# Cross-attention units of a Perceiver layer: the row of maxima on another queue, value products placed later, and the last unit's exponentials

## The chip, the cores and the metric

The kernel runs on one core of a Trainium2 chip. A core has five engines that follow their own instruction streams and meet at semaphores: TensorE (PE, matrix products; its weight loads are listed apart as PEld), VectorE (DVE), ScalarE (ACT), GpSimd (POOL) and SyncE (SP), which computes nothing and issues most of the transfers. ACT can issue transfers as well. Every engine takes its instructions in program order: one that waits holds back all that stand behind it on that engine.

The metric is the device time of one execution in microseconds, the median of several runs.

## The reference

One Perceiver layer over 16 batches of 64 latent rows (1024 wide): cross-attention to a context of 1024 rows for each batch, then self-attention with rotary embedding, then a feed-forward with quantized weights. The change touches the cross-attention and the first steps behind it.

```python
def xattn(query, key, value, Wq, Wk, Wv, Wo):      # 32 heads of 32, 8 key/value heads
    q = (query @ Wq).reshape(b, sq, 32, 32).transpose(0, 2, 1, 3)
    k = (key @ Wk).reshape(b, sk, 8, 32).transpose(0, 2, 1, 3)
    v = (value @ Wv).reshape(b, sk, 8, 32).transpose(0, 2, 1, 3)
    k, v = jnp.repeat(k, 4, axis=1), jnp.repeat(v, 4, axis=1)
    scores = jnp.einsum('bhqd,bhkd->bhqk', q, k) * 32 ** -0.5
    out = jnp.einsum('bhqk,bhkd->bhqd', jax.nn.softmax(scores, -1), v)
    return out.transpose(0, 2, 1, 3).reshape(b, sq, 1024) @ Wo

x = x + xattn(layernorm(x), ctx, ctx, Wq, Wk, Wv, Wo)
x = x + attn(layernorm(x), wq, bq, wk, bk, wv, bv)
x = x + ffn(layernorm(x), w_gate, w_up, w_down, s_gate, s_up, s_down)
```

The context is given transposed, so that its products need no transposition on the chip.

## The kernel before

All data are float32 in one large buffer that the program places by hand (`arena`; the profile names nearly every tile so). The order of instructions is the order of the program text: no scheduler moves anything. PSUM tiles for projections come from a pool of two buffers (`m_tile`), the score tiles from two buffers `w0` and `w1`.

**Units.** The cross-attention is cut into 32 units (class `Unit`, L416). Unit n is batch n // 2 and head group n % 2 (four key/value heads, jj 0 to 3, each shared by four query heads: 256 columns, that is 4 heads x 64 rows). The scores of a unit are held transposed, keys on the partitions, in four quarters of 256 keys. The methods are these:

- `by_key(i)` (L421): eight matmuls for quarter i into `w0` and `w1` (profile: PE t L430), then ACT copies both halves into the quarter's buffer (L442) and DVE keeps the running maximum over the keys, element by element, in `most` (L446 for quarter 0, L449 for the others).
- `reduce` (L451): DVE transposes and reduces `most` to one maximum for each of the 1024 columns (L454 to L461), as a 32 x 32 tile `turned_top`.
- `spread` (L465) writes that tile to a row of DRAM, `tops`, 4 KB; `everywhere` (L469) reads the row back into all 128 partitions as `shift_by`, 512 KB. The second waits for the first to land. Both are issued by ACT. Two rows alternate.
- `exponentials(i)` (L472): DVE subtracts `shift_by` from quarter i (L475), ACT takes the exponential (L476), POOL adds it to `acc`, the sum over keys (L479 for the first addition, L482 for the other six).
- `values(waves)` (L484): 16 matmuls for two quarters, exponentials times values (PE o L491).
- `finish` (L499): four matmuls with ones give the sums (PE o L501), then DVE divides (L508, L513 or L515) and POOL copies one half (L518).

**The unit loop (L919 to L985).** The loop's unit n has its scores already; while its exponentials and value products run, the scores of unit n + 1 (`following`) are made. One pass has four steps i, one for each quarter. Between them the program takes work from a list, `fillers`, with `fill()`: two pieces a step, eight a unit. For units 0 to 29 the list holds the projections of the next batch's context: for an even n its first 512 keys, for an odd n the other 512. They are four half products for the keys (PE k L225; two halves make one product of eight matmuls, copied by ACT at L305) and then four blocks for the values (PE v L311, eight matmuls each, copied by ACT at L318), so that the steps 0 and 1 fill with keys, the steps 2 and 3 with values. For units 30 and 31 it holds 16 halves of the output projection (`project_out`, PE wo L225, with a residual addition on DVE, L529) for the rows of tiles 4, 5, 0 and 1 and, behind tiles 0 and 1, their second layer norm (`norm2`: DVE L170 to L174, POOL L176, DVE L162). `norm2` writes to the places of `most` and `shift_by`.

**Behind the loop (L986 on).** The rest of the list, then the output projections of tiles 2 and 3 with the transpositions of the normed tiles (`transpose2`, PE n2p L260), three pieces of which go ahead of the last unit's `finish`; then tiles 6 and 7, the self-attention and the feed-forward.

**Other transfers.** SP issues the context halves (`load_context`, L207 for all loads by `load`; 2 MB each, two stream buffers, so a load waits for PE to have read the one before the last), the rows of x (L203), and the pieces of the feed-forward's weights, 688 KB each (`load_piece`, L369). Such a piece is treated by ACT on its way through the loop (`treat_piece`, L372): in a first round its magnitudes are summed (L377), in a second it is made ternary (L381, L385), written back by SP (L386), and the piece after the next is loaded. Treatments stand in every step up to unit 7, later in steps 0 and 2, and in step 3 of odd units. Their instructions on ACT stand between the score copies and the projections' copies.

**The start.** The query projections of both halves come first (PE q L225); unit 0's scores are made between the last of them. Then come `spread`, `load_context(1, 0)`, and `everywhere` of unit 0, and four value blocks of batch 0 in a row, before step 0 of unit 0 begins with the keys of batch 1.

Of the kernel before, what the change touches and what calls it, by code (L numbers as in the profile page):

```python
# [20 lines left out]
P = 128  # L21
# [6 lines left out]
HD = 32  # L28
# [21 lines left out]
def kernel(  # L50
# [21 lines left out]
    nc = tc.nc  # L72
# [17 lines left out]
    def m_tile(name):  # L90
        return ps_m.tile([P, 512], F32, tag="m", name=name)
# [4 lines left out]
    def place(kb, shape, dtype=F32):  # L96

        first, n = round(kb * 256), math.prod(shape) * mybir.dt.size(dtype)
        a = arena[:, first : first + (n + 3) // 4]
        if dtype != F32:  # L100
            a = a.bitcast(dtype)
        a = a[:, : math.prod(shape)]
        if len(shape) > 1:
            names = [f"a{i}" for i in range(len(shape))]
            sizes = dict(zip(names[1:], shape[1:]))
            a = a.rearrange(f"p ({' '.join(names)}) -> p {' '.join(names)}", **sizes)
        return a
# [47 lines left out]
    tops = [dram.tile([1, 1024], F32, name=f"tops{i}") for i in range(2)]  # L155

    def layernorm(dst, src, name):

        made = []
        return [  # L160
            lambda: made.append(layernorm_scale(src, name)),
            lambda: nc.vector.tensor_scalar(  # L162
                dst, src, made[0][0][:, 0:1], made[0][1], ALU.subtract, ALU.mult
            ),
        ]
# [26 lines left out]
    shift_by = place(176, [1024])  # L192
# [6 lines left out]
    turned_top = place(195.25, [HD])  # L199
    quarters = most[:, 0:P].rearrange("p (i q) -> p i q", i=4)  # L200

    def load_x(dst, t):
        nc.sync.dma_start(dst, x[bass.ts(t, P), :])  # L203
# [13 lines left out]
    def matmul_steps(out, lhsT, rhs, done):  # L217

        made = []

        def piece(first):
            if first:
                made.append(out())
            for k in range(0, 4) if first else range(4, KC):
                nc.tensor.matmul(  # L225
                    made[0], lhsT=lhsT(k), rhs=rhs(k), start=(k == 0), stop=(k == KC - 1)
                )
            if not first:
                done(made[0])

        return [lambda: piece(True), lambda: piece(False)]
# [22 lines left out]
    def transposed(dst, xn, name, tile, engines):  # L254

        for i in range(2):
            tp = tile(f"{name}_{i}")
            tp = tp.rearrange("p (k q) -> p k q", k=4)
            for k in range(4):
                nc.tensor.transpose(tp[:, k, :], xn[:, bass.ts(i * 4 + k, P)], ident)  # L260
            if engines[i] == "act":
                nc.scalar.copy(dst[i], tp)  # L262
            else:
                nc.vector.tensor_copy(dst[i], tp)
# [25 lines left out]
    def load_context(b, h):  # L290
        ctx_halves[b, h] = load(ctxT[b, h])
# [66 lines left out]
    def half_of(a, c):  # L358
        return a[:, (c % 2) * HALF : (c % 2 + 1) * HALF]
# [5 lines left out]
    def load_piece(i):  # L365
        if i < 2 * len(pieces_of_w):
            m, c = pieces_of_w[i % len(pieces_of_w)]
            st = ws_ring.next([HALF])
            nc.sync.dma_start(st, weight_source(m, c))  # L369
            loaded.append((i, m, c, st))  # L370

    def treat_piece():  # L372
        if not loaded:
            return
        i, m, c, st = loaded.pop(0)
        if i < len(pieces_of_w):
            nc.scalar.activation(st, st, AF.Abs, accum_out=asum[:, m, c : c + 1])  # L377
        else:


            nc.scalar.activation(  # L381
                st, st, AF.Identity, scale=inverse[:, m : m + 1], bias=magic[:, 0:1]
            )
            q = place(ternary_at, [HALF], F8)
            nc.scalar.activation(q, st, AF.Sign, bias=magic[:, 1:2], saturate=False)  # L385
            nc.sync.dma_start(half_of(ternary[m][c // 2], c), q)  # L386
        if i + 2 not in (len(pieces_of_w), len(pieces_of_w) + 1):
            load_piece(i + 2)
# [27 lines left out]
    class Unit:  # L416
# [47 lines left out]

        def spread(self):  # L465
            row = tops[self.n % 2]
            nc.scalar.dma_start(row.rearrange("o (n c) -> (o n) c", n=HD), turned_top[0:HD])

        def everywhere(self):  # L469
            nc.scalar.dma_start(shift_by, tops[self.n % 2].to_broadcast([P, 1024]))  # L470

        def exponentials(self, i):  # L472
            pt = self.pts[i]
# [49 lines left out]
    def project_out(t, h):  # L523
        cols = bass.ts(h, 512)
        return matmul_steps(
            lambda: m_tile(f"wo_{t}_{h}"),
            lambda k: outputs[k // 4][:, t, k % 4, :, :],
            lambda k: wos[h][:, k, :],
            lambda ps: nc.vector.tensor_tensor(xs[t][:, cols], ps, xs[t][:, cols], ALU.add),  # L529
        )  # L530
# [20 lines left out]
    def norm2(t):  # L551
        n2s[t] = n2_ring.next([DIM])
        for step in layernorm(n2s[t], xs[t], f"n2_{t}"):
            step()

    def transpose2(t, tile):
        half, tl = t // 4, t % 4
        cols = bass.ts(tl, P)
        transposed([a[:, :, cols] for a in n2T[half]], n2s[t], f"n2p_{t}", tile, ("act", "dve"))
# [318 lines left out]
    fillers = []  # L878

    def fill(n=1):  # L880
        for _ in range(n):
            if fillers:
                fillers.pop(0)()

    with tc.manual_schedule():
# [14 lines left out]
        unit, last = Unit(0, kT, v), None  # L900
# [12 lines left out]
        unit.spread()  # L913
        load_context(1, 0)
        fillers += value_steps[1]
        unit.everywhere()

        tiles = [(kT, v)]
        for n in range(2 * B):  # L919

            b = n // 2
            if n % 2 == 0:
                fill(len(fillers))
                if b + 1 < B:
                    load_context(b + 1, 1)
                    kT, v, key_steps, value_steps = project(b + 1)
                    tiles.append((kT, v))
                    for h in range(2):
                        fillers += key_steps[h] + value_steps[h]
                else:  # L930
                    for t in range(4):
                        load_x(xs[t], t)
                    nc.sync.dma_start(wkvs2, wkv2)
                    for h in range(2):
                        for t in (4, 5):
                            fillers += project_out(t, h)
                    for t in (0, 1):
                        for h in range(2):
                            fillers += project_out(t, h)
                        fillers += [lambda t=t: norm2(t)]  # L940
            following = Unit(n + 1, *tiles[(n + 1) // 2]) if n + 1 < 2 * B else None

            for i in range(4):
                if following:
                    following.by_key(i)
                    if i == 3:
                        following.reduce()
                if n < 8 or i % 2 == 0 and (n, i) != (8, 0) or i == 3 and n % 2 == 1:
                    treat_piece()
                if n == 8 and i < 2:  # L950
                    (thresholds, thresholds_end)[i]()
                if i == 1 and n % 2 == 1:

                    if b + 2 < B:
                        load_context(b + 2, 0)
                    elif b + 2 == B:
                        wos.append(load(wo[0]))
                fill()
                if i == 1:
                    unit.exponentials(0)  # L960
                if i == 2:
                    unit.exponentials(2)
                    unit.values((0, 1))
                if i == 3:
                    unit.values((2, 3))
                if following and i == 3:
                    following.spread()
                fill()
                if following and i == 3:
                    following.everywhere()  # L970
                if last and i == 0:
                    last.finish()
                if i == 1:
                    unit.exponentials(1)
                if i == 2:
                    unit.exponentials(3)
            if n == 2 * B - 4:
                for t in (4, 5):
                    load_x(xs[t], t)
            if n == 2 * B - 3:  # L980
                wos.append(load(wo[1]))
            if n == 2 * B - 2:
                for t in (6, 7):
                    load_x(xs[t], t)
            last, unit = unit, following  # L985
        fill(len(fillers))  # L986
        for t in (2, 3):
            for h in range(2):
                fillers += project_out(t, h)
            fillers += [lambda t=t: (transpose2(t - 2, m_tile), norm2(t))]  # L990
        fill(3)
        last.finish()
        fill(len(fillers))
        for h in range(2):
# [182 lines left out]
```

## Time and profile before

Three runs gave 1922.90, 1917.52 and 1927.97 us; the median is 1922.9. The profiled execution took 1922.23 us, of which the profile's span covers 1920.4.

| | us | share of the span | instructions |
|---|---|---|---|
| span | 1920.4 | 100% | 26969 |
| PE, matmuls | 1891.1 | 98% | 11392 |
| PEld, weight loads (beside PE) | 1098.6 | 57% | 11392 |
| DVE | 1162.4 | 61% | 1336 |
| ACT | 863.7 | 45% | 932 |
| POOL | 836.7 | 44% | 411 |

The groups of instructions that the change touches or that stand beside it:

| group | count | busy us | mean ns |
|---|---|---|---|
| PE k L225, key projections | 1056 | 470.5 | 598 |
| PE v L311, value projections | 1984 | 460.5 | 385 |
| PE t L430, scores | 2048 | 146.6 | 400 |
| PE o L491, value products | 2048 | 125.3 | 384 |
| DVE L475, subtraction | 128 | 363.8 | 2880 |
| ACT L476, exponential | 128 | 244.7 | 1912 |
| POOL L482, sums | 192 | 574.4 | 2992 |

| transfer | count | KB each | us from issue to landing, median |
|---|---|---|---|
| context half, SP | 31 | 2048 | 8.9 |
| weight piece in_wu, SP | 32 | 688 | 4.2 |
| broadcast of the row, ACT | 32 | 512 | 4.0 |
| row of maxima, ACT | 32 | 4 | 3.1 |

How to read it: a float32 matmul is recorded as two matmul records, and matmuls overlap in the pipeline, so the mean of one is longer than its share of the time; the distance between starts is what counts. "PE t" names the tile that is written, "L430" the line. An arrow `<-` behind a time names what the engine had waited for. SPq and ACTq are the engines' DMA issues. The granted clock of PE is 0.996 of full speed over the span.

### The profile page before, as it was taken

The page shows a single profiled execution, that of the slowest core. Times are in us where ns is not written, and L with a number is a line of the kernel's source. Part 1 is how long each engine was busy: PE and PEld are TensorE (multiplying, and loading weights), DVE is VectorE, ACT ScalarE, POOL GpSimd, SP SyncE. Part 2 cuts the span into 40 slices and gives each one's busy share as a digit, 9 for nine tenths or more (in the row PEclk, how much of TensorE's full clock was granted, in tenths as well). Part 3 has the DMA queues.
Part 4 walks back from the last instruction along what each step waited for, and adds up shares of the span by engine and source line. Part 5 has one row for each costly group of instructions (what it writes and reads, how often), then busy time and mean ns, then how long its engine had stood idle before and what let it go on. Part 6 is the DMA issues. An engine that isn't in the chain of part 4 may idle for free.

```text
span 1920.4 us, 26969 instructions
## 1 busy us (share of the span) xinstructions
PE 1891.1 (98%) x11392; PEld 1098.6 (57%) x11392; DVE 1162.4 (61%) x1336; ACT 863.7 (45%) x932; POOL 836.7 (44%) x411
## 2 busy tenths in 40 slices
PE   8999999999999999999999999999899999999999
PEld 5445566556656655665665566555346465566654
DVE  3012777677777767777776777677533235666565
ACT  1243565566566666666765666554100012233110
POOL 1000466456546644664564466456501424444430
PEclk9999999999999999999999999999999999999999
DMA  8224353343342343333333433314002001034334
GB/s 336 74 89 168 100 177 135 134 173 114 114 173 102 120 165 112 129 119 145 122 111 121 173 111 111 139 56 165 11 4 88 0 1 42 21 86 115 100 77 111
DMA packets 79177, 213.37 MB, mean 111 GB/s; under 512 B 38288, under 2 KB 47440, under 8 KB 74064
## 3 DMA queue, kind: packets, MB, share of 16 engines
q1 hardware_dynamic: 71760, 192.64, 29.9%
q10 hardware_dynamic: 7296, 19.01, 2.9%
q8 instruction: 89, 1.46, 0.3%
q14 instruction: 32, 0.26, 0.0%
HBM read 190.98 MB, written 12.78 MB: 106 GB/s over the span
## 4 chain that ended last, share of the span: by engine, by line
PE 82%; DVE 10%; ACT 3%; DMA 3%; issue 1%; POOL 0%; ACTq 0%; DVEq 0%; POOLq 0%
PE k L225 19%; PE v L311 18%; PE q L225 12%; PE t L430 6%; PE wo L225 5%; PE o L491 5%; DVE arena L475 4%; PE gu L806 4%; PE d L865 3%; PE g L806 3%; DMA tops<-arena 2%; DVE arena L449 2%; ACT arena L476 1%; PE v L589 1%; ACT arena L442 1%
## 5 line engine op out<-in xcount | busy, mean ns | idle before, releaser
L482 POOL TENSOR_TENSOR arena<-arena 128x1024 f32<-128x1024 f32 x192 | 574.4, 2992 | 24.5 <-ACT arena L476 9.4
L225 PE MATMUL k<-arena 128*128 128x512 f32 x1056 | 470.5, 598 | 0.0
L311 PE MATMUL v<-arena 128*128 128x256 f32 x1984 | 460.5, 385 | 0.0
L311 PEld LDWEIGHTS v<-arena 128*128 128x128 f32 x1984 | 367.0, 190 | 90.1 <-issue 45.1
L475 DVE TENSOR_TENSOR arena<-arena 128x2048 f32<-128x2048 f32 x128 | 363.8, 2880 | 0.0
L479 POOL TENSOR_TENSOR arena<-arena 128x1024 f32<-128x1024 f32 x32 | 77.7, 2427 | 649.4 <-ACT arena L476 529.5
L449 DVE TENSOR_TENSOR arena<-t,arena 128x512 f32<-128x512 f32 x384 | 262.1, 689 | 150.3 <-ACT arena L442 99.1
L225 PEld LDWEIGHTS k<-arena 128*128 128x128 f32 x1056 | 195.3, 190 | 241.0 <-issue 234.3
L476 ACT ACTIVATE arena<-arena 128x2048 f32<-128x2048 f32 x128 | 244.7, 1912 | 176.6 <-DVE arena L475 176.6
L442 ACT COPY arena<-t 128x1024 f32<-128x1024 f32 x256 | 249.0, 1012 | 166.9 <-DMA tops<-arena 92.1
L225 PE MATMUL q<-arena 128*128 128x512 f32 x512 | 227.6, 600 | 0.6 <-ACT arena L262 0.6
L446 DVE TENSOR_REDUCE arena<-t 128x512 f32<-128x1024 f32 x64 | 78.1, 1224 | 210.5 <-PE t L430 119.5
L225 PEld LDWEIGHTS q<-arena 128*128 128x128 f32 x512 | 96.2, 192 | 117.4 <-issue 115.1
L430 PE MATMUL t<-arena 32*128 32x256 f32 x2048 | 146.6, 400 | 4.6 <-DVE arena L446 4.6
L430 PEld LDWEIGHTS t<-arena 32*128 32x128 f32 x2048 | 92.5, 184 | 68.5 <-issue 49.1
L491 PE MATMUL o<-arena 128*32 128x256 f32 x2048 | 125.3, 384 | 6.0 <-ACT arena L476 6.0
L806 PEld LDWEIGHTS <-arena 128*128 128x128 bf16 x1024 | 98.2, 97 | 54.8 <-issue 5.4
L225 PE MATMUL wo<-arena 128*128 128x512 f32 x256 | 115.0, 605 | 0.0
L818 POOL TENSOR_TENSOR arena<-arena 128x344 f32<-128x344 f32 x64 | 70.8, 1109 | 98.5 <-DVE arena L815 89.0
L318 ACT COPY arena<-v 128x256 f32<-128x256 f32 x124 | 45.9, 370 | 117.1 <-DVE arena L461 82.5
L508 DVE RECIPROCAL arena<-o 128x256 f32<-128x256 f32 x32 | 56.2, 1755 | 65.9 <-PE o L501 65.9
L491 PEld LDWEIGHTS o<-arena 128*32 128x32 f32 x2048 | 59.8, 110 | 63.2 <-issue 17.6
(120 smaller groups left out, 1492.0 us busy)
## 6 DMA issues: line engine op xcount, KB each, us to landing
arena<-in_ctxT SPq DMA_DIRECT2D x31, 2048.0 KB, 8.9
arena<-in_wg SPq DMA_DIRECT2D x32, 688.0 KB, 4.3
arena<-in_wu SPq DMA_DIRECT2D x32, 688.0 KB, 4.2
arena<-in_wd SPq DMA_DIRECT2D x32, 688.0 KB, 4.1
arena<-tops ACTq DMA_DIRECT2D x32, 512.0 KB, 4.0
arena<-ternary SPq DMA_DIRECT2D x32, 344.0 KB, 3.4
ternary<-arena SPq DMA_DIRECT2D x48, 172.0 KB, 1.9
arena<-in_x SPq DMA_DIRECT2D x16, 512.0 KB, 11.1
```

Source lines behind the costliest of these rows:

```text
L225: nc.tensor.matmul(made[0], lhsT=lhsT(k), rhs=rhs(k), start=(k == 0), stop=(k == KC - 1))
L311: nc.tensor.matmul(ps[:, :KVD], lhsT=ctx_halves[b, h][:, k, bass.ts(kt, P)], rhs=wkvs[:, k, KVD:], start=(k == 0), stop=(k == KC - 1),)
L430: nc.tensor.matmul(ws[jj // 2][:, jj % 2, a, :], lhsT=self.kT[rows, self.g, bass.ts(i * 2 + a, P)], rhs=qa[self.g][rows, bass.ts(self.b, 2 ...
L442: nc.scalar.copy(pt[:, 2 * mine : 2 * mine + 2], ws[mine])
L446: nc.vector.tensor_reduce(m, w.rearrange("p j a c -> p j c a"), AX.X, ALU.max)
L449: nc.vector.tensor_tensor(m, w[:, :, a], m, ALU.max)
L475: nc.vector.tensor_tensor(pt, pt, by.to_broadcast([P, 4, 2, 256]), ALU.subtract)
L476: nc.scalar.activation(pt, pt, AF.Exp)
L479: nc.gpsimd.tensor_tensor(acc, pt[:, :, 0], pt[:, :, 1], ALU.add)
L482: nc.gpsimd.tensor_tensor(acc, acc, pt[:, :, a], ALU.add)
L491: nc.tensor.matmul(self.po[bass.ts(jj, HD), 0:256], lhsT=self.v[:, kt, bass.ts(self.g * 4 + jj, HD)], rhs=self.pts[i][:, jj, a, :], start= ...
L806: nc.tensor.matmul(ps[:, :CW], lhsT=xqT[t][:, k, :], rhs=wbs[n][i][:, k, :], start=(k == 0), stop=(k == KC - 1),)
```

## The change

Three things are changed in the text.

`spread` now issues the row's write and the broadcast's read one after the other, both from SP; `everywhere` is gone. In the loop it stands in step 3 behind the weight piece's treatment, ahead of the first `fill()`; at the start it stands ahead of `load_context(1, 0)` as before, now with the broadcast.

`values` of a step, in steps 2 and 3, stands behind both `fill()` of that step instead of between them.

The last unit (no `following`) has its own order: quarter 0's exponentials at the end of step 0, behind the `finish` of unit 30; quarter 1's between the two pieces of step 1; quarters 2 and 3 behind them. `norm2` of tiles 0 and 1 leaves the list of units 30 and 31 and stands behind the loop, each behind one half of tile 2's output projection; five pieces instead of three go ahead of the last `finish`.

```diff
         def spread(self):
             row = tops[self.n % 2]
-            nc.scalar.dma_start(row.rearrange("o (n c) -> (o n) c", n=HD), turned_top[0:HD])
-
-        def everywhere(self):
-            nc.scalar.dma_start(shift_by, tops[self.n % 2].to_broadcast([P, 1024]))
+            nc.sync.dma_start(row.rearrange("o (n c) -> (o n) c", n=HD), turned_top[0:HD])
+            nc.sync.dma_start(shift_by, tops[self.n % 2].to_broadcast([P, 1024]))
...
         unit.spread()
         load_context(1, 0)
         fillers += value_steps[1]
-        unit.everywhere()
...
                     for t in (0, 1):
                         for h in range(2):
                             fillers += project_out(t, h)
-                        fillers += [lambda t=t: norm2(t)]
...
                 if n < 8 or i % 2 == 0 and (n, i) != (8, 0) or i == 3 and n % 2 == 1:
                     treat_piece()
+                if following and i == 3:
+                    following.spread()
...
                 fill()
-                if i == 1:
-                    unit.exponentials(0)
-                if i == 2:
-                    unit.exponentials(2)
-                    unit.values((0, 1))
-                if i == 3:
-                    unit.values((2, 3))
-                if following and i == 3:
-                    following.spread()
+                if i in (1, 2) and following:
+                    unit.exponentials(2 * i - 2)
+                if i == 1 and not following:
+                    unit.exponentials(1)
                 fill()
-                if following and i == 3:
-                    following.everywhere()
                 if last and i == 0:
                     last.finish()
-                if i == 1:
-                    unit.exponentials(1)
-                if i == 2:
+                    if not following:
+                        unit.exponentials(0)
+                if i in (1, 2) and following:
+                    unit.exponentials(2 * i - 1)
+                if i == 1 and not following:
+                    unit.exponentials(2)
                     unit.exponentials(3)
+                if i > 1:
+                    unit.values((2 * i - 4, 2 * i - 3))
...
         for t in (2, 3):
             for h in range(2):
                 fillers += project_out(t, h)
+                if t == 2:
+                    fillers += [lambda h=h: norm2(h)]
             fillers += [lambda t=t: (transpose2(t - 2, m_tile), norm2(t))]
-        fill(3)
+        fill(5)
         last.finish()
         fill(len(fillers))
```

## The prediction, made before the changed kernel had run

> **What bounds the kernel now.** I read the busy shares first, then the chain that ended last, then who waits for whom, and last the order of time in one unit, at the start and at the end of the unit loop.
>
> ```profile
> PE 1891.1 (98%) x11392; PEld 1098.6 (57%) x11392; DVE 1162.4 (61%) x1336; ACT 863.7 (45%) x932; POOL 836.7 (44%) x411
> PE 82%; DVE 10%; ACT 3%; DMA 3%; issue 1%; POOL 0%; ACTq 0%; DVEq 0%; POOLq 0%
> ```
>
> PE is busy 98% of the span. The chain's 10% on DVE and 3% on DMA do not say that PE stood: in most units those steps and PE end together. The waits tell how long it stood (columns: microseconds in total, times, longest):
>
> ```profile
> ACT arena L442 <- DMA tops<-arena: 92.1, 19, 6.5
> ...
> PE o L491 <- ACT arena L476: 6.0, 3, 5.0
> ...
> PE t L430 <- DVE arena L446: 4.6, 7, 0.9
> ```
>
> So ACT stands 92.1 us behind the row of maxima, but PE pays 4.6 us for it. The loop is bound by PE's own stream. The chain in order of time (start, length) shows the second half of unit 0:
>
> ```profile
> 203.02 3.65 PE v L311 x16
> 206.67 1.86 PE o L491 x32
> 208.54 3.65 PE v L311 x16
> 212.19 1.08 PE t L430 x16
> ```
>
> One unit is 2 key products of 7.06, four value projections of 3.65, two value products of 1.86, four score blocks of 1.08 and 0.57 for the sums (L501): 37.33 us. The chain's first key product starts at 861.57, 898.90 and 936.24, which is that period: there is no idle in it.
>
> **Part 1: value products at the end of their quarter.** The order v, o, v, t becomes v, v, o, t, twice a unit. What is a v beside a v worth? The timeline has four in a row, before unit 0; each is followed by its copy, which starts 0.10 us after the block's end (the last ends at 185.60, where the score block starts):
>
> ```profile
> 175.34 0.37 ACT L318 COPY arena<-v 128x256 f32<-128x256 f32 x1 [1.53 <-PE v L311]
> 178.80 0.37 ACT L318 COPY arena<-v 128x256 f32<-128x256 f32 x1 [3.08 <-PE v L311]
> ...
> 185.70 0.37 ACT L318 COPY arena<-v 128x256 f32<-128x256 f32 x1 [3.08 <-PE v L311]
> ```
>
> They are 3.45 us apart (the third copy, left out here, starts at 182.25); a v after a t or an o takes 3.65. Each join saves 0.20. Does o followed by t cost more than o followed by v? No t follows L491 before, but L501, of the same shape, lasts 0.57 before a t (230.57) and before an output product (1399.52): equal. So 2 x 0.20 = 0.40 us a unit. Unit 30 has output products there; two halves cost 3.62 apart and 7.06 joined, again about 0.2. Sum: 31 x 0.40 = **-12.4 us**. From both sides: nothing, if o before t takes it back; -16 if the chain's 13.81 for the four is compared with 4 x 3.65 (0.26 a join).
>
> What this uncovers: v needs a PSUM buffer of two that alternate. The first v of a fourth quarter needs the second-last v's copy (at 922.5 where PE comes at 925.7); the next unit's key product needs the copy that ends at 934.03 and would start at 935.8. The products come later than now, which gives exponentials more room. Order on DVE, ACT and POOL within the loop is unchanged apart from the two DMA issues.
>
> **Part 2: row and broadcast on SP.** Off ACT go 32 row writes and 32 broadcasts, and the waits for the reduction and for the row. The timeline of one unit boundary:
>
> ```profile
> 935.24 0.33 ACTq L467 DMA_DIRECT2D tops<-arena  x1
> 940.45 0.33 ACTq L470 DMA_DIRECT2D arena<-tops  x1
> 940.87 1.93 ACT L442 COPY arena<-t 128x1024 f32<-128x1024 f32 x2 [4.89 <-DMA tops<-arena]
> ```
>
> The copies of score block 0 wait 4.89 us, DVE's maxima wait for them, and in seven units the next score block waits for DVE. After the change they start with the score block or with the end of POOL's adds (936.7), so maxima end near 940.3 where PE needs them at 943.4. The seven PE waits go. In the chain's key-product starts those seven units lengthen their spans by 0.90, 0.89, 1.00, 0.61, 0.74, 0.69, 0.25: **-5.1 us**.
>
> Is the shift now late? Before, it takes 5.2 us to the second issue and 4.2 to landing: 944.7, against the first subtraction (DVE L475), which starts at 948.72. After, the row stands in SP's queue behind a weight piece (in every unit up to the eighth, in every second one later; here it is issued at 934.2, and 4.1 us is the median to its landing). The Trainium skill ("DMA: Bandwidth & Descriptors", section "Queues, rings and completion order") says that an engine takes turns between queue rows, packet by packet. By that rule the change is bad: ACT's own row let 4 KB slip between large loads, on SP's it queues behind them. But here the row with its own queue still took 1.3 us alone and 5.2 to 6.8 beside the context load that SP issues at the same moment. After, that load stands behind the broadcast. By the rule the row becomes 4.1 later; by the rows it lands near 939.7 instead of 940.4, and the broadcast near 944. Either way the subtraction, 13.1 us after the reduction, isn't met. What SP holds back meanwhile: the context load, 5 us later with 37 us until use; the next weight piece, used two treatments on; stores that ACT gates later anyway. Cost nothing.
>
> One place has no such cover: before unit 0 the context of batch 1 is queued behind both.
>
> ```profile
> 168.77 5.40 SPq L369 DMA_DIRECT2D arena<-in_wu  x2
> 174.26 11.76 SPq L207 DMA_DIRECT2D arena<-in_ctxT  x2
> ```
>
> It is issued at 174.26, lands after 9.5 to 9.9, and PE needs it at 186.67. After, SP issues the row at 174.3 behind a piece issued at 173.8 (landing 177.9), row down by 175.7 to 179.3, broadcast, context issued 176.4 to 179.7. Landing takes 7.8 to 9.7, with up to 1.2 for 512 KB ahead at the 450 GB/s of that stretch: 184 (no cost) to 190.6 (4.0). I take 189, nearer the late end because the piece is certainly ahead: **+2.3 us**.
>
> **Part 3: the last unit.** Its subtractions are now issued between other work; norm2(0) stands on DVE between the second and third.
>
> ```profile
> 1362.35 1.07 PE L491 MATMUL o<-arena 128*32 128x256 f32 x16
> 1368.42 1.93 PE L491 MATMUL o<-arena 128*32 128x256 f32 x16 [5.00 <-ACT arena L476]
> 1370.29 9.11 PE L225 MATMUL wo<-arena 128*128 128x512 f32 x16
> ```
>
> The same stretch in windows (start and end, length, busy time of the five engines, then the granted clock as the third number from the end):
>
> ```profile
> 1370.00:1374.00 4.00, 4.00 (x9) 1.65 (x6) 0.12 (x1) 0.00 (x0) 3.76 (x3) 0.50 0.00 0
> ```
>
> From 1362.35 to 1370.29 is 7.94 for a product of 1.87; the output product takes 9.04 (to 1379.33) instead of 7.06, since the granted clock is 0.50 from 1368 to 1374; the last pair, to 1382.09 and with another 0.69 behind ACT, 2.76 instead of 1.87. Sum 6.07 + 1.98 + 0.89 = 8.9 us. After: subtraction 0 at 1357.6 as now, 1 right behind it (1360 to 1362.3), 2 and 3 after one residual add (1363.1 to 1369.8), exponentials done by 1371.8. The first product comes at 1369.4, the second at 1378: neither waits. POOL's seven adds (2.4 + 6 x 3.1 = 21 us from 1361.9) end at 1382.8, the sums come 11 us later. norm2(0) and norm2(1) move behind: some 3.5 us each on DVE; the first has the 7 us of the output product ahead of its transposition, the second 14 us. With unit 30's wait of 0.28: **-9.2 us**.
>
> **Sum.** -12.4 - 5.1 + 2.3 - 9.2 = -24.4 on the profiled execution's 1922.2: 1897.8, which I call **1898**. The median of the runs is 0.7 us above that execution, which is below their spread of 10 us.
>
> The clock weighs on the start: the skill ("TensorE: Matmul & The Clock Gate", Part 1, "What's actually happening") has PE at half rate after one idle window of about 3.4 us. The 5.00 above bought 1.98 more, which fits. With my 2.3 the rule adds nothing, at the late end of 4.0 it adds about 2: that bound becomes +6.
>
> **Rivals.**
> - *Joins pay nothing* (12%): PE's switch cost appears elsewhere. For it: no o-before-t of this form exists. Against: L501. 1922.2 - 12.0 = 1910.
> - *The row comes too late on SP* (8%, the slower side): from the reduction the subtraction stands 13.1 us off, and POOL's adds leave PE another 3.3, so delay decides from 16.4 us on; then each us costs 31. The longest row seen (6.8) with the longest broadcast (9.7) is 16.5, so it would need both in every unit. At 18 us: 1898 + 31 x 1.6 = 1948. Faster turns into slower at about 17.2.
> - *A new wait in the loop takes half the gain* (6%): a PSUM copy behind ACT's exponentials and weight pieces, whose room is 1.7 us; 0.6 us in each of 30 units gives 1916, which could not be told from no change.
>
> The forecast has the remaining 74%, its own range 1890 to 1907 (joins 0.12 to 0.26, start 0 to +6, run spread). With the joins' rival the range is 1889 to 1914. About 0.5% (9.6 us) is what can be told from no change: faster 0.85, same 0.07, slower 0.08.
>
> **What would show it.** Two v blocks 7.10 us long as one piece, key products 36.93 apart; no PE wait on L446 and no ACT wait on tops; a wait of PE k for in_ctxT near 187, up to 4 us; no half clock near 1368, no PE wait on L476. Key products still 37.3 apart would break part 1; subtractions waiting on the broadcast would break part 2.

## The result and the profile after

The changed kernel takes 1893.5 us in the median (1892.95 to 1893.80) against 1922.85 before, a ratio of 0.985 with a 95% interval of 0.982 to 0.987. The profiled execution took 1893.80 us, its span is 1892.0, that is 28.4 us less than before. From the page of the changed kernel, the busy shares and the chain by engine:

```profile
PE 1872.4 (99%) x11392; PEld 1101.6 (58%) x11392; DVE 1162.1 (61%) x1336; ACT 865.6 (46%) x932; POOL 841.1 (44%) x411
PE 97%; DVE 1%; DMA 1%; ACT 0%; issue 0%; POOL 0%; DVEq 0%; ACTq 0%
```

The other engines do the same work in the same time; the chain is now almost wholly PE's. Its course over one unit in the changed kernel (start, length, what):

```profile
898.09 7.06 PE k L225 x16
905.16 1.08 PE t L430 x16
906.23 7.10 PE v L311 x32
913.34 1.86 PE o L489 x32
915.20 1.08 PE t L430 x16
916.28 7.10 PE v L311 x32
923.38 1.86 PE o L489 x32
925.25 1.08 PE t L430 x16
926.32 7.06 PE k L225 x16
```

Two value blocks are one piece of 7.10 us, where they were two of 3.65, and the value product before a score block still takes 1.86. The first key product of one unit starts at 889.38 and that of the next at 926.32: 36.94 us, against 37.33. What PE still waits for in the changed kernel (total, times, longest), from the list of its waits:

```profile
PE k_first L331 <- DMA arena<-in_ctxT: 5.4, 1, 5.4
...
PE k L225 <- DMA arena<-in_ctxT: 0.9, 1, 0.9
```

No wait behind L446 is left, and none behind an exponential. The two traces are compared below at four instructions that both have: the first key product of batch 1, the first output product, the first transposition of a normed tile, the first gate product (differences of starts rounded to 0.1 us).

| stretch | before, us | after, us | difference | forecast |
|---|---|---|---|---|
| to the first key product | 186.7 | 188.1 | +1.4 | +2.3 |
| units 0 to 29 | 1124.5 | 1107.5 | -17.0 | -17.1 |
| units 30, 31 and the first tiles' output | 92.4 | 82.7 | -9.7 | -9.6 |
| from there to the first gate product | 252.6 | 249.4 | -3.2 | 0 |
| feed-forward | 264.2 | 264.3 | +0.1 | 0 |

Of the first +1.4, PE's wait for the context is 0.93; 0.4 had come about by 172 us, ahead of anything that the change touches. The fourth stretch runs the same instructions in both kernels; its 3.2 us are taken up below, with the scatter.

### The profile page after: what moved, and what is told of

Read it like the earlier page. It is cut to its first block, busy times and chain, and to the rows that moved or that the text cites. A ratio compares the mean times of both kernels' runs of the same rounds, so it can differ in the third digit from the quotient of the medians.

```text
span 1892.0 us, 26992 instructions
## 1 busy us (share of the span) xinstructions
PE 1872.4 (99%) x11392; PEld 1101.6 (58%) x11392; DVE 1162.1 (61%) x1336; ACT 865.6 (46%) x932; POOL 841.1 (44%) x411
## 4 chain that ended last, share of the span: by engine, by line
PE 97%; DVE 1%; DMA 1%; ACT 0%; issue 0%; POOL 0%; DVEq 0%; ACTq 0%
PE k L225 25%; PE v L311 23%; PE q L225 12%; PE t L430 7%; PE o L489 6%; PE wo L225 6%; PE gu L804 4%; PE d L863 4%; PE g L804 3%; PE v L587 1%; PE o L499 1%; PE k_first L331 1%; PE w L627 1%; PE v_first L339 1%; DMA arena<-in_ctxT 1%; PE w L691 0%
## 5 line engine op out<-in xcount | busy, mean ns | idle before, releaser
L311 PE MATMUL v<-arena 128*128 128x256 f32 x1984 | 444.4, 382 | 0.0
L311 PEld LDWEIGHTS v<-arena 128*128 128x128 f32 x1984 | 372.0, 190 | 68.5 <-issue 20.0
L446 DVE TENSOR_REDUCE arena<-t 128x512 f32<-128x1024 f32 x64 | 75.4, 1219 | 109.3 <-PE t L430 109.3
L569 POOL TENSOR_TENSOR arena<-arena 128x512 f32<-128x512 f32 x20 | 35.5, 1774 | 123.0 <-DVE arena L567 123.0
```

The costliest lines, as they stand in the source:

```text
L311: nc.tensor.matmul(ps[:, :KVD], lhsT=ctx_halves[b, h][:, k, bass.ts(kt, P)], rhs=wkvs[:, k, KVD:], start=(k == 0), stop=(k == KC - 1),)
```

## The experiments

### One part at a time

Three kernels have one part of the change each. The first moves the row and its broadcast to SP, at the place that they have in the changed kernel.

```diff
-            nc.scalar.dma_start(row.rearrange("o (n c) -> (o n) c", n=HD), turned_top[0:HD])
...
-            nc.scalar.dma_start(shift_by, tops[self.n % 2].to_broadcast([P, 1024]))
+            nc.sync.dma_start(row.rearrange("o (n c) -> (o n) c", n=HD), turned_top[0:HD])
+            nc.sync.dma_start(shift_by, tops[self.n % 2].to_broadcast([P, 1024]))
```

> The kernel before with the queue change alone (row and broadcast on SP, in step 3 behind the weight piece). Own theory: the seven waits of PE L430 behind DVE L446 go (-5.1 us), the start pays 0.9 us for the context behind the row: about 1918.6 us against 1922.85; units stay 37.33 us apart, the last unit keeps its 5 us wait. Rival (the freed ACT is what made the changed kernel fast): 1905 us or less, and units shorter than 37.3.

Measured: 1916.76 us, ratio 0.9964 (0.9952 to 0.9976). In its trace units 0 to 29 take 1119.4 us, 5.1 less than before; no wait of PE behind L446 is left, pairs of value blocks are two pieces of 3.65 us, and the last unit keeps its 5.0 us. So the freed ACT, which stood 92.1 us before, is worth 5.1 us by itself. That the freed ACT alone made the kernel fast, the rival, is refuted: the units keep their 37.33 us.

The second moves the value products.

```diff
                 if i == 2:
                     unit.exponentials(2)
-                    unit.values((0, 1))
-                if i == 3:
-                    unit.values((2, 3))
...
                 if i == 2:
                     unit.exponentials(3)
+                if i > 1:
+                    unit.values((2 * i - 4, 2 * i - 3))
```

> The kernel before with the value products at the end of their quarter alone. Own theory: pairs of value blocks take 7.10 us as one piece (-12 us), but the row still holds ACT up, and since PE now comes 0.4 us earlier to the next unit, its waits behind L446 grow by 0.4 us each and more units have them: 4.6 us before, 8 to 13 us here; total -4 to -9, that is 1914 to 1919 us. Rival (the parts add up independently): waits stay near 4.6 us, total -12.4, 1910.5 us. Second rival (the gain of this part is room for the exponentials, not the join): pairs still 7.3 us.

Measured: 1917.21 us, ratio 0.9968 (0.9957 to 0.9978). Pairs are pieces of 7.10 us, but the list of waits of this kernel has

```profile
PE t L430 <- DVE arena L446: 12.5, 12, 1.9
```

instead of 4.6 in seven. Units 0 to 29 take 1120.6 us: 3.9 less, near the 4.1 that 12.0 for the joins less 7.9 of new waits would give. This is where the parts meet. The joins bring PE to the next unit's second score block earlier, and there ACT still stands behind the row (90.6 us in all in this kernel). Alone the two parts save 5.1 + 3.9 = 9.0 us in these units, together 17.0: the move of the row is worth 13.1 us where the products have been moved.

The third rearranges the last unit and the two norms.

```diff
...
                     last.finish()
-                if i == 1:
+                    if not following:
+                        unit.exponentials(0)
+                if i == 1 and following:
                     unit.exponentials(1)
-                if i == 2:
+                if i == 1 and not following:
+                    unit.exponentials(2)
+                    unit.exponentials(3)
+                if i == 2 and following:
                     unit.exponentials(3)
...
+                if t == 2:
+                    fillers += [lambda h=h: norm2(h)]
...
-        fill(3)
+        fill(5)
```

> The kernel before with the last unit's exponentials in a row and the two norms behind the loop, alone. Own theory: no wait of PE on L476 in the last unit and no half clock there, -9 us: 1914 us; units 37.33 us apart, waits behind L446 as before (4.6 us). On the clock of the self-attention stage there are two theories: if the 5 us idle of the last unit also makes the later dips of the granted clock (0.95 and 0.94 between 1600 and 1660 us of the span before), they are gone here, the gain is 12 us and the runs agree within 2 us; if the dips hang on where a window of the clock falls by chance, they come and go from run to run, and the runs scatter by 3 to 10 us as those of before do.

Measured: 1912.25 us, ratio 0.9948 (0.9934 to 0.9962). The 5.0 us wait and the half clock of the last unit are gone; waits behind L446 are 4.0 us in six. From the first output product to the first transposition it takes 83.4 us against 92.4, the 9 us expected. On the clock the runs spoke for chance: with the last unit's idle gone, six runs still scatter from 1910.84 (mean granted clock 1.000) to 1917.17 (0.998).

As whole runs the three parts save 0.36%, 0.32% and 0.52%, 1.2% in all, against 1.5% for the change. That fits a gain that only the parts together have, but the intervals (0.1 to 0.3 points on either side) are too wide to settle it; the stretches of the traces do.

### How late may the shift be?

The rival on the slower side put the point from which a late row costs time at 16.4 us behind the reduction. The changed kernel's trace suggested a smaller room: from the first subtraction to the next reduction DVE and ACT work in one chain, so the row's way and that chain close a ring. Two kernels repeat the broadcast, each waiting for the one before it: one twice, as below, the other three times.

```diff
-            nc.sync.dma_start(shift_by, tops[self.n % 2].to_broadcast([P, 1024]))
+            for _ in range(2):
+                nc.sync.dma_start(shift_by, tops[self.n % 2].to_broadcast([P, 1024]))
```

> The changed kernel with the broadcast of every row issued twice, the second behind the landing of the first: the shift lands some 4.2 us later in every unit (10 to 12 us behind the reduction instead of 5.8 to 7.5). Both theories of the room: no unit gets longer (36.94 us), since the first subtraction stands 13.1 us behind the reduction. The start pays 4 us for the context behind it, perhaps 2 more for the clock: 1898 to 1900 us.

> The changed kernel with every broadcast issued three times: the shift lands 14 to 16 us behind the reduction, later than the first subtraction. Theory of the prediction (PE has another 3.3 us behind the subtraction, delay decides from 16.4 us on): units stay 36.94 us, only the start pays 8 to 10 us, about 1903 us. Rival (a ring: from the first subtraction to the next reduction DVE and ACT take 23.8 us in a chain with no room, so that the period cannot be below the row's way plus 23.8): units get 1 to 3 us longer, 38 to 39.8 us, 40 to 80 us in all, 1945 to 1985 us.

Measured: 1899.5 us with two broadcasts, 1917.83 with three (1914.49 to 1922.94). With two, the key products stand 36.94 apart as in the changed kernel, and the start pays: PE waits 3.8 us there, with half clock behind it, which makes units 0 to 29 3.0 us longer (1110.5 against 1107.5). With three, units 0 to 29 take 8.8 us more than with two, and the start waits 7.8. The other 10 us between the two spans are 5.2 at the start, 1.7 in the stretch behind the units, where PE waits 1.6 us for a weight load (Wo), and 3.3 of granted clock in the self-attention. The chain of the kernel with three (start, length, what):

```profile
905.58 1.32 DMA tops<-arena
906.92 3.71 DMA arena<-tops
910.64 3.89 DMA arena<-tops
914.55 3.87 DMA arena<-tops
...
918.51 2.30 DVE arena L474
...
942.36 3.36 DMA tops<-arena
945.73 3.68 DMA arena<-tops
949.43 3.68 DMA arena<-tops
953.13 4.26 DMA arena<-tops
```

The chain has no matmul here: it goes from row to broadcast to the subtraction (918.51) and through DVE and ACT to the next row, 942.36. From subtraction to row it is 23.85 us, a chain with no room in it; the row's way is 12.9 us in one unit and 15.1 in the next, behind a weight piece. The ring's period is therefore some 37.9 us in these two units, in the mean, above PE's 36.94. The rows' issues from 566 to 1206 us stand 38.7 and 36.4 us apart in turn, a mean of 37.6. So there is no second reserve of 3.3 us: a mean way of 14.0 us, which is below 16.4, already costs PE time, and the two-broadcast kernel's, some 10 us as an estimate from its issues, does not. The sum 36.94 - 23.85 puts the end of the room between them, at 13.1 us, taken as a mean over the units. The size in the rival's expectation (40 to 80 us) was too large: the third broadcast takes 3.7 us rather than 4.2, in the later units half of the rows have no weight piece directly ahead, and up to 610 us PE still keeps its 36.94 us from unit to unit.

### The row behind the large load

The row of every second unit now stands right behind `load_context(b + 1, 1)` on SP.

```diff
+                if n:
+                    unit.spread()
...
-                if following and i == 3:
+                if following and i == 3 and n % 2 == 0:
                     following.spread()
```

> The changed kernel with the row of every second unit (those at a change of batch) issued behind the 2 MB context load on SP instead of ahead of it. Own theory: SP's transfers are served in their order, so the row takes 8 to 9 us (8.2 behind the context at the start of the kernel with the context first) instead of 2.6, and the shift lands 12.5 to 14 us behind the reduction, at or behind the first subtraction (13.1) in every second unit; but the ring of row, DVE and reduction counts over two units (14 and 6 us, mean 10, under 13.1), so that units stay 36.94 us and the kernel 1893 to 1898 us. Rival (each late shift costs PE its lateness, or the load costs more than its own time): 38 us or more in every second unit, 1905 us or more.

Measured: 1894.51 us, ratio 0.987 (0.985 to 0.989). SP's part of the timeline in this kernel:

```profile
925.04 0.39 SPq L207 DMA_DIRECT2D arena<-in_ctxT  x1
925.57 0.32 SPq L467 DMA_DIRECT2D tops<-arena  x1
934.02 0.33 SPq L468 DMA_DIRECT2D arena<-tops  x1
...
962.52 0.32 SPq L467 DMA_DIRECT2D tops<-arena  x1
963.86 0.32 SPq L468 DMA_DIRECT2D arena<-tops  x1
```

Behind 2 MB on the same queue the 4 KB take 8.45 us, alone 1.34; up to 10.0 in this kernel. DVE waits for the broadcast in six units, 3.9 us in all, and PE in none: units 0 to 29 take 1107.5 us, to the tenth those of the changed kernel. A shift that came later than the subtraction in six units cost PE nothing, since the ring's mean still had room.

### The context first, and the scatter

PE's 0.9 us wait at the start goes when the load changes places with the row.

```diff
-        unit.spread()
         load_context(1, 0)
+        unit.spread()
```

> The changed kernel with the context load of batch 1 ahead of unit 0's row on SP. Own theory: the 0.9 us wait of PE for the context at 188 us goes, the row lands behind 2 MB near 184 and the broadcast near 188, still 9 us before the first subtraction: 1892.6 us. Rival (row and broadcast become late and hold unit 0 up): 1894 us or more, with DVE L473 of unit 0 waiting for the broadcast.

> The changed kernel once more, beside the one with the context first, for the scatter of both. If the granted clock falls by chance in stages that both kernels share, the runs scatter over 1892 to 1898 us, as those of the kernel with the context first did. If the changed kernel is free of it, they stay within 1 us of 1893.5.

> The changed kernel with the context load of batch 1 ahead of unit 0's row, once more, beside the changed kernel on the same chip. Own theory: 0.9 us less in the trace at the start, no wait of PE for in_ctxT, and both kernels scatter alike by the clock, so that the medians differ by less than the scatter. Rival (the later row costs something): slower by over 2 us in the median.

Measured: 1896.51 us (1892.11 to 1898.16) and, repeated, 1895.89 (1895.36 to 1898.32); the changed kernel beside it 1893.95 (1892.38 to 1897.23). The wait is gone from both traces, and the kernel is not faster. The runs follow their mean granted clock: with 1.000 the changed kernel took 1892.4 to 1893.8 us and the kernel with the context first 1892.1; with 0.998 the one took 1897.2 and the other 1895.8 and 1896.0, and with 0.997 the other took 1898.1 to 1898.3. What is gained at the start is smaller than this scatter. The rival, over 2 us for the later row, is not excluded by the medians (1.94 apart), but the traces show no wait for it: units 0 to 29 take 1107.5 us in both, as in the changed kernel, and what both lose, 1.6 us, lies in the stretch ahead of the first gate product. Why the context first draws the lower clock more often (seven of its eight runs at 0.999 or less, two of eight of the changed kernel) isn't explained. It does not beat the changed kernel, and nothing else that was tried does.

The same scatter accounts for the 3.2 us of the fourth stretch. The timeline of PE in the self-attention, before:

```profile
1626.19 3.10 PE L629 MATMUL w<-arena 32*128 32x64 f32 x64 [1.84 <-DVE arena L735]
1629.22 9.35 PE L225 MATMUL q<-arena 128*128 128x512 f32 x16
```

and the same place in the changed kernel:

```profile
1600.94 2.01 PE L627 MATMUL w<-arena 32*128 32x64 f32 x64 [1.84 <-DVE arena L733]
1602.89 7.13 PE L225 MATMUL q<-arena 128*128 128x512 f32 x16
```

PE has stood 1.84 us in both. In the one the matmuls then take 12.4 us to the end of the query product, in the other 9.1: 3.3 us. The windows of the two kernels (start and end, length, busy time of the five engines, granted clock third from the end) say why. Before, and then after:

```profile
1620.00:1640.00 20.00, 16.73 (x100) 9.08 (x98) 11.65 (x15) 1.76 (x4) 8.68 (x7) 0.83 0.08 14
```

```profile
1590.00:1610.00 20.00, 18.16 (x170) 9.52 (x168) 12.68 (x18) 3.59 (x6) 8.23 (x6) 1.00 0.08 15
```

In windows of 2 us the clock before is 0.50 from 1628 to 1632. A mean of 0.83 over 20 us is then 6.8 us at half rate.

The other nine traces have the same gap of 1.84 us at the same place, and windows of 2 us there show that the loss comes in steps: none in six of the eleven traces (this stretch then takes 249.4 us), 3.4 us at half rate in three (251.0 us), 6.8 in two (252.6 and 252.7 us). By the same windows it begins 1.4 us behind the gap's end in the three, 0.7 and 0.4 us in the two. The kernel with only the row moved keeps the last unit's idle and has no loss here, and those with the context first or with three broadcasts lack that idle and have one: the idle of the last unit does not decide it.

## Why the prediction was right, step by step

**The joins** were sized from four value blocks that stood in a row before unit 0. The pair measures 7.10 us and the period 36.94, both as forecast; that the sums' product L501 speaks for L491 ahead of a score block held too. Why a block of another kind costs 0.20 us more is not shown.

**The row on SP.** The waits of PE went, and 17.0 us in units 0 to 29 stand against 17.1. The sum took 5.1 for the seven waits of before; the single kernels show that this is the price only beside the old order of products. With the joins the stall would have grown to 12.5 us; the sum was right because it counted the joins in full and removed the stall in full. The unit boundary that the prediction looked at, in the changed kernel (timelines of SP, ACT and DVE):

```profile
925.70 0.32 SPq L467 DMA_DIRECT2D tops<-arena  x1
928.99 0.33 SPq L468 DMA_DIRECT2D arena<-tops  x1
...
926.41 1.01 ACT L442 COPY arena<-t 128x1024 f32<-128x1024 f32 x1 [1.64 <-PE t L430]
...
938.80 4.48 DVE L473 TENSOR_TENSOR arena<-arena 128x2048 f32<-128x2048 f32 x2
```

The row behind a weight piece takes 3.3 us and, with 4.2 for the broadcast, the shift lands some 7.5 us behind the reduction; the forecast had 8.7. The subtraction starts 13.1 us behind it, as forecast. POOL's adds do not hold the copies up, as was thought: the copies start when the score block has ended (926.33), ahead of the end of POOL's adds (927.15), and in no unit do they wait for POOL any more. So the maxima end 5 us before PE needs them instead of 3.

**The start** was the mis-sized term: +2.3 in the sum, 0.9 measured as a wait. SP's timeline and, last, the chain in the changed kernel:

```profile
174.69 0.38 SPq L467 DMA_DIRECT2D tops<-arena  x1
178.66 0.34 SPq L468 DMA_DIRECT2D arena<-tops  x1
...
179.09 8.88 DMA arena<-in_ctxT
```

The row landed at 178.66, near the late end of the 175.7 to 179.3 that were forecast. But the context load, with the broadcast ahead of it, then took 8.88 us, where up to 10.9 (9.7 and 1.2) had been allowed; it landed at 187.97 and not at 189. The 0.9 us had no half clock behind them. For a wait near 4 us the prediction had put the half clock at about 2 us; the kernel with two broadcasts paid 3.0 for it.

**The last unit** came out at -9.7 with unit 30's join, against -9.6. Its subtractions run in pairs from 1341.31 and 1346.82, its products follow the output products without a wait, and the half clock went with the idle: the output product between the value products takes 7.1 us instead of 9.1.

```profile
1352.97 1.93 PE L489 MATMUL o<-arena 128*32 128x256 f32 x32
1354.84 7.13 PE L225 MATMUL wo<-arena 128*128 128x512 f32 x16
1361.90 1.93 PE L489 MATMUL o<-arena 128*32 128x256 f32 x32
```

**The rival on the slower side** had its point in the wrong place. It added 3.3 us behind the subtraction, read from PE's next need. But a unit's lateness comes back through its own maxima to the next reduction, so that reserve can be spent once, in the first units, and not in every one. The ring's sum puts the point at 13.1 us of mean way, between the kernels with two and with three broadcasts. The chance was small for the right reason all the same: by the changed kernel's rows (1.3 to 4.8 us) and the 4.2 us of a broadcast in the median, the way is some 5.5 to 9 us.

**What the sum left out** is the clock: 3.2 us of the profiled difference belong to the granted clock in a stretch that the change does not touch. That they fell to the changed kernel's side is luck, not forecast. With the start's +1.4 in place of +2.3, and 0.1 of the smaller terms the other way, they make up the 4.0 us by which the sum of 1897.8 lies above the profiled 1893.8.

## What to carry to other kernels

Where one engine is busy without a gap, look at what it pays for changing the kind of its work: here a value block beside another saved 0.20 us, twice in each of 31 units. A wait on another engine is worth what the bounding engine waits because of it, but that price holds only for the present order: move the bounding engine forward, and waits that were hidden come out. For a chain that passes from one round of a loop into the next, take its whole way round and compare it with the period; room that is counted at one point and not round the ring is not there in every round.

## What the hardware showed unexpectedly

- Half clock by chance. The same gap of 1.84 us, with the same instructions around it, was followed by full rate in six traces, by 3.4 us at half rate in three and by 6.8 us in two. The Trainium skill ("TensorE: Matmul & The Clock Gate") tells of windows of about 3.4 us that run freely (Part 1, "What's actually happening") and advises against idle gaps of over some 3 us ("Why this matters for your kernels"). The steps of 3.4 us agree with the windows; the advice is not enough here, since a gap below a window's length was not safe. What decides wasn't found: no run shifted the phase on purpose, and whether the gap alone counts, or also the small products behind it, wasn't tested.
- It makes runs of one kernel scatter. Twenty runs of the kernel before lay between 1919.92 and 1932.40 us, the longest with a mean granted clock of 0.994, the shortest with 0.998.
- On one queue, 4 KB behind a larger load landed late: they took 1.3 us alone, 3.2 to 4.8 when issued 1.1 us behind 688 KB, and 8.2 to 10.0 when issued 0.5 to 1.4 us behind 2 MB. On a queue of their own beside the same 2 MB they had taken 5.1 to 6.8, so that a queue of its own had not spared the row the large load either.
